# A four-layer graph network on one core: when the experts' weights are turned, and where layer 0's keys, values and context are computed

## The chip, the cores and the metric

The kernel runs on one NeuronCore of a Trainium2 chip. A core has five engines, each with its own in-order queue: TensorE (matmuls; its loads of stationary operands are listed apart as PEld), VectorE (DVE in the profile), ScalarE (ACT), GpSimd (POOL) and SyncE (SP), which here only starts transfers. Sixteen DMA engines move data. The metric is the device time of one execution in microseconds (us).

## The reference

A graph of 3125 nodes with 256 features and 103,125 edges passes through four layers. Each layer normalizes its rows, adds a graph attention and a "mix" (some form of global attention), normalizes again and adds a feed-forward part. Two places matter here.

Layer 0's mix, as this kernel computes it from the normalized rows `xn` and the weight matrix `Wqkv` (256 x 768):

```python
q, k, v = xn @ Wqkv                    # 256 columns each
context = softmax(k over nodes).T @ v  # by head, 32 x 32 in each of 8 heads
gate    = sigmoid(gelu(ln(xn) @ Wg1 + bg1) @ Wg2 + bg2)
x      += (gate * (q @ context)) @ Wproj + bproj
```

The kernel multiplies the query weights with the context once (a 256 x 256 matrix that it calls `fold`), so that `q @ context` is one product `xn @ fold`.

Layer 1's feed-forward part:

```python
shared  = relu(relu(x @ sW1 + sb1) @ sW2 + sb2) @ sW3 + sb3
w       = weights of the top 2 of 4 experts, from softmax(x @ gW + gb)
out     = shared + sum_e w[e] * (relu(relu(x @ eW1[e] + eb1[e]) @ eW2[e] + eb2[e]) @ eW3[e] + eb3[e])
```

## The kernel before

**Tiles.** The 3125 rows lie in 25 tiles of 125 rows (`NT`, `TP`). Tiles are taken in seven `GROUPS`: four of four tiles (500 columns when turned) and three of three (375). `x` holds the rows, `xn` the normalized rows and `xT` the same turned, as two blocks of 128 features by 3125 columns.

**The order of the work.** The code states what depends on what and in which order it is written; a planner then puts the instructions of each engine into a fixed order, by an estimate of when each could start, and by the order in the code where several could. It also places the semaphores. On the chip each engine follows that order strictly: an instruction that waits holds all behind it on its engine. Transfers start from the queues of SP, ScalarE and GpSimd. A pool with `bufs=2` gives a name two buffers in turn, and a third use waits until the first buffer's readers are done. PSUM, where matmuls write, is shared by the pools of a stage.

**The beginning.** `run` (L2479 on) loads `x`, and `begin_layer` normalizes all seven groups and turns them into `xT`. Then `prepare` checks that the graph has a form for which the fast layers hold. VectorE compares the first target of each of 3224 rows of edges with five sets of first nodes (L1381, 125 x 3224 each), and GpSimd gathers 256 edges for each of 625 sets of nodes from memory (five indirect transfers, L1387). VectorE turns these into a low digit and a key for each edge, which go to memory (`seg_d`), counts what it found, bounds the attention scores by products of `xT` with the attention vectors (L1437 to L1439), bounds the key weights (`w_k`), and writes one word `ok`. All engines read `ok` (`values_load`), and a branch takes either the fast layers or a general path. Nothing of the fast layers can be moved before the branch by the planner.

**Layer 0's counts.** `counts` (L1480) builds, for the 625 sets of five nodes, how many edges lead from each node to each. It works in 63 steps of ten sets: VectorE makes two one-hot arrays in bf16 (`oh_lo`, L1515, and `oh_key`, L1518, two buffers each), TensorE multiplies them (`p_cnt`, L1530, 20 matmuls a step), ScalarE copies the counts to bytes (`stage`, L1532), and each 250 columns go to memory. Beside it runs a generator, `mix0_pieces`, of which pieces are taken between the steps:

```python
while done < (g0 // B + 1) * PIECES0 // steps:
    next(work, None)
    done += 1
```

`PIECES0` is 107, just as many as there are: one for the weights, 25 for keys, values and context (one for each tile: a product with 512 columns, exp of the keys, a copy of the values, two context products that add up over all tiles in `p_ctx`), one for `fold`, 42 for the gate and the output (six for each group), and 38 for `node_pieces`, which make the attention's node tables `zs` and `bar` and the queries `q_d`. After the loop, `dense_pairs` reads the counts back (`a`) and multiplies.

**Layer 1's feed-forward.** `ffn1` goes through the groups. `before(i + 1)` turns group i+1 (`transposed`, into `p_tr`), computes its router scores, takes softmax and top 2 on VectorE (some 25 short operations, with ScalarE's exp between), and turns the resulting weights `wf` so that they lie as 5 x 500 (L1056 to L1058). Then group i's shared network runs (`h1`, `h2`), then its four experts in two pairs, each pair masked by a product of `own` with the turned weights (`p_e`, L1086), and at last `p_y`, which adds shared part, experts and biases. `p_tr`, `p_e` and `p_y` have two PSUM buffers each.

Of the kernel before, what the change touches and what calls it, by code (L numbers as in the profile page):

```python
# [10 lines left out]
F32 = mybir.dt.float32  # L11
# [30 lines left out]
KEYS = HI * GN  # L42
PIECES0 = 107
SC = 8
# [5 lines left out]
GROUPS = [(0, 4), (4, 4), (8, 4), (12, 4), (16, 3), (19, 3), (22, 3)]  # L50
# [6 lines left out]
class Net:  # L57
# [976 lines left out]
    def ffn1(self, x, xn, xT, weights):  # L1034
        nc, tc = self.nc, self.tc
        E = 4
        with ExitStack() as s:
            c = s.enter_context(tc.tile_pool(name="f1", bufs=1))
# [4 lines left out]
            wfs = {}  # L1043

            def before(i):
                if i < len(GROUPS):
                    t0, nt = g = GROUPS[i]
                    self.transposed(ps, xT, xn, groups=[g])
                    wf = self.top2(wr, self.softmax(wr, self.scores(wr, ps, xT[:, :, t0 * TP:(t0 + nt) * TP], nt, gw, gb)))

                    more = wr.tile([TP, nt, E + 1], F32, name="wf_1")
                    nc.vector.memset(more[:, :, E:], 1.0)
                    nc.vector.tensor_copy(more[:, :, :E], wf)
                    p = ps.tile([P, 512], F32, name="p_tr")[:E + 1]
                    for t in range(nt):
                        nc.tensor.transpose(p[:, t * TP:(t + 1) * TP], more[:, t, :], self.ident[:TP, :TP])  # L1056
                    wfs[i] = wr.tile([E + 1, 512], F32, name="wf_t")
                    nc.scalar.activation(wfs[i][:, :nt * TP], p[:, :nt * TP], AF.Copy)  # L1058

# [3 lines left out]
            for i, (t0, nt) in enumerate(GROUPS):  # L1063
                before(i + 1)
                wf = wfs[i]
                n = nt * TP
# [8 lines left out]
                self.mm(p[:, :n], [(s2[:, k, :], h1[:, k, :n]) for k in range(KC)])  # L1075
                nc.scalar.activation(h2[:, :n], p[:, :n], AF.Relu, bias=sb2[:, 0:1], scale=1.0)
                pairs = []
                for j in range(E // 2):
# [272 lines left out]
class Dense(Net):  # L1351
# [8 lines left out]
    def prepare(self, pool, xT):  # L1360
# [6 lines left out]
        with ExitStack() as s:  # L1367
# [18 lines left out]
            for b in range(GN):  # L1386
                nc.gpsimd.indirect_dma_start(out=seg[:, b, :], out_offset=None, in_=ins["segments"],  # L1387
                                             in_offset=bass.IndirectOffsetOnAxis(ap=at_i[:, b:b + 1], axis=0))
            lo = w.tile([TP, GN, SEG], F32, name="seg_lo")
            key = w.tile([TP, GN, SEG], F32, name="seg_key")  # L1390
# [37 lines left out]
            nc.vector.tensor_reduce(found[:, 1:2], above, AX.X, OP.add)  # L1428
            p_f = ps.tile([1, 2], F32, name="p_f")
            nc.tensor.matmul(p_f, self.ones[:, 0:1], found, start=True, stop=True)  # L1430


            gw = self.gnn_weight(w, ps, "g0", 8)
            ends = w.tile([16, 2, len(GROUPS)], F32, name="ends")
# [30 lines left out]
            nc.vector.tensor_mul(self.ok, ok[:, 0:1], ok[:, 2:3])  # L1465
        return self.ok

# [4 lines left out]
    def counts(self, pieces):  # L1472
# [5 lines left out]
        with ExitStack() as s:  # L1478
# [5 lines left out]
            with tc.tile_pool(name="cnti", bufs=1) as wi, tc.tile_pool(name="cntt", bufs=2, space=PSUM) as ps:  # L1484
                for i, name in enumerate(("lo_t", "key_t")):
# [57 lines left out]
    def mix0_pieces(self, x, xn, xT, nodes, c, w):  # L1543
# [3 lines left out]
        with ExitStack() as s:  # L1547
            ps = s.enter_context(tc.tile_pool(name="m0p", bufs=3, space=PSUM))
            ps1 = s.enter_context(tc.tile_pool(name="m0p1", bufs=1, space=PSUM))
            wqkv = self.weight(c, "L0_mix_Wqkv")  # L1550
            wproj = self.weight(c, "L0_mix_Wproj")
# [3 lines left out]
            bg1, bg2 = self.vec(c, "L0_mix_bg1", rows=64), self.vec(c, "L0_mix_bg2")  # L1555
            bproj = self.row(c, "L0_mix_bproj")
            nc.gpsimd.tensor_add(x, x, bproj[:, None, :].to_broadcast([TP, NT, C]))
            p_ctx = [ps1.tile([P, P + 1], F32, name=f"p_ctx{m}") for m in range(KC)]
            yield
            for t in range(NT):  # L1560
                p = ps.tile([TP, 2 * C], F32, name="p_a")
                self.mm(p, [(xT[:, k, t * TP:(t + 1) * TP], wqkv[:, k, C:]) for k in range(KC)])
                ek = w.tile([TP, C], F32, name="ek", bufs=2)
                nc.scalar.activation(ek, p[:, :C], AF.Exp)
                v = w.tile([TP, KC, P + 1], F32, name="v", bufs=2)
                nc.scalar.activation(v[:, :, :P], p[:, C:].rearrange("p (m f) -> p m f", m=KC), AF.Copy)
                nc.gpsimd.memset(v[:, :, P], 1.0)
                for m in range(KC):
                    nc.tensor.matmul(p_ctx[m], ek[:, m * P:(m + 1) * P], v[:, m, :], start=(t == 0), stop=(t == NT - 1))
                yield  # L1570

            inv = w.tile([P, KC], F32, name="inv")
            ctxt = w.tile([P, KC, P], F32, name="ctxt")
            for m in range(KC):
                nc.vector.reciprocal(inv[:, m:m + 1], p_ctx[m][:, P:])
                nc.vector.scalar_tensor_tensor(ctxt[:, m, :], p_ctx[m][:, :P], inv[:, m:m + 1], self.heads, op0=OP.mult, op1=OP.mult)
            fold = c.tile([P, KC, C], F32, name="fold")
            for k in range(KC):
                p = ps.tile([P, 512], F32, name="p_a")
                for m in range(KC):  # L1580
                    nc.tensor.transpose(p[:, m * P:(m + 1) * P], wqkv[:, k, m * P:(m + 1) * P], self.ident)
                wt = w.tile([P, C], F32, name="wq_t")
                nc.vector.tensor_copy(wt, p[:, :C])
                p = ps.tile([P, 512], F32, name="p_a")
                for m in range(KC):
                    nc.tensor.matmul(p[:, m * P:(m + 1) * P], wt[:, m * P:(m + 1) * P], ctxt[:, m, :], start=True, stop=True)
                nc.vector.tensor_copy(fold[:, k, :], p[:, :C])
            yield
            for t0, nt in GROUPS:
# [876 lines left out]
    def run(self, x_in, out):  # L2466
# [195 lines left out]
```

## Time and profile before

| | |
|---|---|
| median of 3 runs | 5535.72 us (5531.63 to 5546.36) |
| profiled execution | 5533.53 us, span 5531.5 us |
| mean granted TensorE clock | 0.938 |
| start to `ok` | 92.1 us |
| from `ok` to the end of the counts and node tables | 92.1 to 392.2 us |
| layer 1's feed-forward part | 2682 to 2928 us |

The span runs from the first instruction to the last; the profiled execution's own time is 2.0 us longer. A row of the profile gives source line, engine and operation, then the tiles as output <- input with the partitions and elements of each; idle time before an instruction is put down to the semaphore that came last. `<-issue` is idle time in which nothing visible was waited for. The granted clock is TensorE's, as a share of full speed. A matmul on f32 data appears as two records; the ends of pipelined matmuls are modelled.

### The profile page before, as it was taken

How to read it: one execution, taken by the hardware profiler on the slowest of the kernel's cores; microseconds unless marked ns; L12 is line 12 of the kernel's file. 1: busy time of each engine (PE TensorE's matmuls, PEld its weight loads, DVE VectorE, ACT ScalarE, POOL GpSimd, SP SyncE). 2: the span in 40 equal slices, each digit the busy share in tenths (PEclk: the TensorE clock that was granted, in tenths of full speed). 3: DMA queues.
4: the chain of work that ended last, by engine and by line, in shares of the span. 5: the costliest groups of instructions: out<-in, count | busy, mean ns of one | idle time of the engine just before them, and what ended most of it. 6: DMA issues, size and time to landing. Idle time of an engine off the chain costs nothing. (4 is left out here: it accounts for less than half of the span.)

```text
span 5531.5 us, 66568 instructions
## 1 busy us (share of the span) xinstructions
PE 4813.9 (87%) x24758; PEld 2824.0 (51%) x24758; DVE 3733.4 (67%) x5901; ACT 1034.3 (19%) x1984; POOL 1041.6 (19%) x1185
## 2 busy tenths in 40 slices
PE   4978888879788899989889899979998878989878
PEld 2652234448645433368544433345565555655557
DVE  7789999985565699845333899932223888777753
ACT  2540010011142100110123000023333110333221
POOL 1000000004300000000001100000001777777743
PEclk7999999989899999999889999979999888999989
DMA  3462222232300011111000011120002556666645
GB/s 87 36 68 67 77 63 67 67 116 63 99 19 0 27 34 41 32 39 36 24 1 4 28 33 34 26 71 0 0 1 59 161 164 193 183 173 178 175 149 170
DMA packets 294339, 395.81 MB, mean 72 GB/s; under 512 B 124175, under 2 KB 228000, under 8 KB 293435
## 3 DMA queue, kind: packets, MB, share of 16 engines
q1 hardware_dynamic: 203408, 161.12, 12.7%
q0 software_dynamic: 52528, 167.17, 10.7%
q10 hardware_dynamic: 38072, 63.16, 3.6%
q8 instruction: 202, 3.31, 0.3%
q14 instruction: 129, 1.06, 0.1%
HBM read 345.14 MB, written 49.35 MB: 71 GB/s over the span
## 5 line engine op out<-in xcount | busy, mean ns | idle before, releaser
L1699 DVE SCALAR_TENSOR_TENSOR pt<-q_head,bar,a 128x750 f32<-128x750 f32 (+5 forms) x1200 | 1483.3, 1298 | 80.4 <-PE acc L1804 57.3
L1954 POOL DMA_INDIRECT z_edge<-tab,src_i x806 | 778.0, 965 | 266.9 <-issue 206.4
L1748 PE MATMUL acc<-pt,zs 128*64 128x500 f32 (+2 forms) x2800 | 591.1, 548 | 152.0 <-DVE pt L1699 127.2
L1799 PE MATMUL acc<-pt,zs 128*64 128x375 f32 (+2 forms) x3200 | 604.9, 501 | 25.4 <-DVE pt L1699 25.0
L2022 PE MATMUL p_acc<-z_edge,oh 128*125 128x264 f32 x2044 | 539.9, 425 | 91.7 <-DVE z_edge L2013 91.7
L2022 PEld LDWEIGHTS p_acc<-z_edge,oh 128*125 128x125 f32 x2044 | 419.8, 209 | 191.3 <-DVE z_edge L2013 101.2
L1748 PEld LDWEIGHTS acc<-pt,zs 128*64 128x64 f32 (+1 forms) x2800 | 244.4, 136 | 483.3 <-DVE pt L1699 328.7
L1799 PEld LDWEIGHTS acc<-pt,zs 128*64 128x64 f32 (+1 forms) x3200 | 244.9, 136 | 362.0 <-issue 224.7
L1215 DVE SCALAR_TENSOR_TENSOR x<-p_y,sm,x 125x256 f32<-125x256 f32 x200 | 93.9, 484 | 427.0 <-PE p_y L716 427.0
L1804 PE MATMUL acc<-pt,zs 128*32 128x375 f32 (+2 forms) x3200 | 313.4, 497 | 0.0
L1850 PE MATMUL acc<-zs,pt 128*125 128x257 f32 x1250 | 275.7, 383 | 11.8 <-DMA a<-count_d 11.8
L1850 PEld LDWEIGHTS acc<-zs,pt 128*125 128x125 f32 x1250 | 234.8, 189 | 52.7 <-issue 14.6
L2013 DVE TENSOR_TENSOR z_edge<-z_edge,near_e 128x2112 f32<-128x2112 f32 (+1 forms) x101 | 236.5, 2342 | 17.4 <-ACT near_e L2005 17.4
L1210 ACT ACTIVATE h<-p_tr,bn 128x500 f32<-128x500 f32 (+1 forms) x224 | 161.5, 722 | 357.6 <-PE p_tr L716 357.6
L716 PE MATMUL p_y<-w_L_ffn_Wo,h 128*125 128x256 f32 x800 | 203.7, 387 | 0.0
L1699 DVE SCALAR_TENSOR_TENSOR pt<-q_all,bar,a 128x500 f32<-128x500 f32 (+3 forms) x175 | 119.0, 682 | 122.9 <-PE acc L1850 120.4
L716 PE MATMUL p_tr<-h,w_L_ffn_W 128*128 128x500 f32 (+1 forms) x448 | 191.6, 551 | 7.8 <-ACT h L1210 4.7
L2362 POOL CAST one_e<-one 125x96 bf16<-125x96 f32 (+1 forms) x2 | 2.1, 1049 | 1013.5 <-DVE one L653 1013.5
L716 PE MATMUL p_tr<-xT,w_L_ffn_W 128*128 128x500 f32 (+1 forms) x448 | 190.0, 547 | 0.0
L1804 PEld LDWEIGHTS acc<-pt,zs 128*32 128x32 f32 (+1 forms) x3200 | 85.0, 109 | 203.0 <-issue 201.7
L716 PEld LDWEIGHTS p_y<-w_L_ffn_Wo,h 128*125 128x125 f32 x800 | 144.9, 187 | 73.4 <-ACT h L1210 27.1
L1967 DVE TENSOR_TENSOR hot<-row,near 125x1024 f32<-125x1024 int16 (+1 forms) x149 | 157.6, 1083 | 4.5 <-DMA row<-dst_row 2.9
(513 smaller groups left out, 6696.0 us busy)
## 6 DMA issues: line engine op xcount, KB each, us to landing
row<-dst_row SPq DMA_DIRECT2D x101, 224.0 KB
a<-count_d SPq DMA_DIRECT2D x96, 203.1 KB
a<-count_d SPq DMA_DIRECT2D x96, 187.5 KB
a<-count_d SPq DMA_DIRECT2D x144, 93.8 KB
ef<-in_edge_s SPq DMA_DIRECT2D x101, 128.0 KB
z_edge<-tab,src_i POOLq DMA_INDIRECT x806
count_d<-stage SPq DMA_DIRECT2D x12, 781.2 KB
q_head<-q_g ACTq DMA_DIRECT2D x24, 375.0 KB
```

What stands on the lines that cost most here:

```text
L716: self.nc.tensor.matmul(p, a, b, start=(i == 0), stop=(i == len(pairs) - 1))
L1210: nc.scalar.activation(o[:, m, :n], p[:, :n], AF.Relu, bias=b[:, e, m:m + 1], scale=g[:, e, m:m + 1])
L1215: nc.vector.scalar_tensor_tensor(x[:, t0 + t, :], q, wf[:, t, e:e + 1], x[:, t0 + t, :], op0=OP.mult, op1=OP.add)
L1699: self.nc.vector.scalar_tensor_tensor(pt[:K, :n], q, bar, a[:K, :n], op0=OP.max, op1=OP.mult)
L1748: nc.tensor.matmul(acc[64 * i:64 * i + 64, :b1 - b0], zs[:K, t, z:z + 64], pts[i][:K, b0:b1], start=(t == 0), stop=(t == NS - 1))
L1799: nc.tensor.matmul(acc[i // 2][64 * (i % 2):64 * (i % 2) + 64, b, :b1 - b0], zs[:K, t, i * W:i * W + 64], pts[i][:K, b0:b1], **st)
L1804: nc.tensor.matmul(acc[2][32 * i:32 * i + 32, b, :b1 - b0], zs[:K, t, z:z + 32], pts[i][:K, b0:b1], **st)
L1850: nc.tensor.matmul(acc[i], pt[:K, i * TP:(i + 1) * TP], zs[:K, t, :C + 1], start=(t == 0), stop=(t == NS - 1))
L1954: nc.gpsimd.indirect_dma_start(out=zs[i][:, j, :], out_offset=None, in_=table, in_offset=bass.IndirectOffsetOnAxis(ap=src[:, c0 + j:c0 + j ...
L1967: nc.vector.tensor_tensor(hots[i, t][:, q0 * 256:q1 * 256], rows[i][:, q0 * 256:q1 * 256], node[:, t:t + 1].to_broadcast([TP, (q1 - q0) * ...
L2013: nc.vector.tensor_mul(zh, zh, weight[:, :, :, None].to_broadcast([P, n, H, D + 1]))
L2022: nc.tensor.matmul(acc[t], ohs[i, t][:, k - a, :], zs[i][:, k - c0, :HW], start=(k == cols[t][0]), stop=(k == cols[t][1] - 1))
```

## The change

Four edits.

1. In `ffn1` the turning of the router's weights (transposes, and the copy by ScalarE) leaves `before(i + 1)` and becomes `turned(i)`, called behind group i's shared network.
2. A new function `begin` takes the place of `begin_layer` and the call of `prepare` in `run`. `prepare` is now a generator with two stops. `begin` runs it to the first stop (the gathers), then normalizes and turns group by group, and computes keys, values and context for each group's tiles; after the third group's turning it runs `prepare` to its second stop. Then come `fold`, which is written to memory, and the rest of `prepare`.
3. `mix0_pieces` loses keys, values, context and `fold`, and reads `fold` from memory. `PIECES0` becomes 69, while 81 pieces are left, so that 12 follow the loop. PSUM pools `cntp` and `m0p` go from three buffers to four.
4. In `mix0_pieces` the scaled copy of the turned rows `xnnT` goes from VectorE to ScalarE.

```diff
-PIECES0 = 107
+PIECES0 = 69
...
@@ ffn1, in before(i)
-                    more = wr.tile([TP, nt, E + 1], F32, name="wf_1")
-                    nc.vector.memset(more[:, :, E:], 1.0)
-                    nc.vector.tensor_copy(more[:, :, :E], wf)
-                    p = ps.tile([P, 512], F32, name="p_tr")[:E + 1]
-                    for t in range(nt):
-                        nc.tensor.transpose(p[:, t * TP:(t + 1) * TP], more[:, t, :], self.ident[:TP, :TP])
-                    wfs[i] = wr.tile([E + 1, 512], F32, name="wf_t")
-                    nc.scalar.activation(wfs[i][:, :nt * TP], p[:, :nt * TP], AF.Copy)
+                    wfs[i] = wr.tile([TP, nt, E + 1], F32, name="wf_1")
+                    nc.vector.memset(wfs[i][:, :, E:], 1.0)
+                    nc.vector.tensor_copy(wfs[i][:, :, :E], wf)
+
+            def turned(i):
+                nt = GROUPS[i][1]
+                p = ps.tile([P, 512], F32, name="p_tr")[:E + 1]
+                for t in range(nt):
+                    nc.tensor.transpose(p[:, t * TP:(t + 1) * TP], wfs[i][:, t, :], self.ident[:TP, :TP])
+                wf = wr.tile([E + 1, 512], F32, name="wf_t")
+                nc.scalar.activation(wf[:, :nt * TP], p[:, :nt * TP], AF.Copy)
+                return wf
...
                 before(i + 1)
-                wf = wfs[i]
...
                 nc.scalar.activation(h2[:, :n], p[:, :n], AF.Relu, bias=sb2[:, 0:1], scale=1.0)
+                wf = turned(i)
...
@@ prepare: a stop behind the five gathers, another ahead of p_f; p_f and p_gw take the name p_e
+            yield
...
+            yield
-            p_f = ps.tile([1, 2], F32, name="p_f")
+            p_f = ps.tile([1, 2], F32, name="p_e")
...
-            gw = self.gnn_weight(w, ps, "g0", 8)
+            gw = self.gnn_weight(w, ps, "g0", 8, "p_e")
...
+    def begin(self, pool, x, xn, xT):
+        nc, tc = self.nc, self.tc
+        self.fold_d = self.dram.tile([P, KC * C], F32, name="fold_d")
+        with ExitStack() as s:
+            c = s.enter_context(tc.tile_pool(name="c0", bufs=1))
+            w = s.enter_context(tc.tile_pool(name="c0w", bufs=2))
+            pst = s.enter_context(tc.tile_pool(name="c0t", bufs=2, space=PSUM))
+            ps = s.enter_context(tc.tile_pool(name="c0p", bufs=2, space=PSUM))
+            ps1 = s.enter_context(tc.tile_pool(name="c0c", bufs=1, space=PSUM))
+            checks = self.prepare(pool, xT)
+            next(checks)
+            wqkv = self.weight(c, "L0_mix_Wqkv")
+            p_ctx = [ps1.tile([P, P + 1], F32, name=f"p_ctx{m}") for m in range(KC)]
+            self.layernorm(xn, x, GROUPS[0])
+            for i, (t0, nt) in enumerate(GROUPS):
+                self.transposed(pst, xT, xn, groups=[GROUPS[i]])
+                if i + 1 < len(GROUPS):
+                    self.layernorm(xn, x, GROUPS[i + 1])
+                if i == 2:
+                    next(checks)
+                for t in range(t0, t0 + nt):
+                    p = ps.tile([TP, 2 * C], F32, name="p_a")
+                    self.mm(p, [(xT[:, k, t * TP:(t + 1) * TP], wqkv[:, k, C:]) for k in range(KC)])
+                    ek = w.tile([TP, C], F32, name="ek")
+                    nc.scalar.activation(ek, p[:, :C], AF.Exp)
+                    v = w.tile([TP, KC, P + 1], F32, name="v")
+                    nc.scalar.activation(v[:, :, :P], p[:, C:].rearrange("p (m f) -> p m f", m=KC), AF.Copy)
+                    nc.gpsimd.memset(v[:, :, P], 1.0)
+                    for m in range(KC):
+                        nc.tensor.matmul(p_ctx[m], ek[:, m * P:(m + 1) * P], v[:, m, :], start=(t == 0), stop=(t == NT - 1))
...
+            nc.sync.dma_start(self.fold_d, fold.rearrange("p k f -> p (k f)"))
+            for _ in checks:
+                pass
...
@@ counts
-            ps = s.enter_context(tc.tile_pool(name="cntp", bufs=3, space=PSUM))
+            ps = s.enter_context(tc.tile_pool(name="cntp", bufs=4, space=PSUM))
...
@@ mix0_pieces: the 25 tiles of keys, values and context and the making of fold are gone
-            wqkv = self.weight(c, "L0_mix_Wqkv")
...
+            fold = c.tile([P, KC, C], F32, name="fold")
+            nc.sync.dma_start(fold.rearrange("p k f -> p (k f)"), self.fold_d)
...
-                    nc.vector.tensor_scalar(xnnT[:, k, :n], p[:, :n], g[:, k:k + 1], b[:, k:k + 1], op0=OP.mult, op1=OP.add)
+                    nc.scalar.activation(xnnT[:, k, :n], p[:, :n], AF.Identity, bias=b[:, k:k + 1], scale=g[:, k:k + 1])
...
@@ run
-        self.begin_layer(x, xn, xT)
-        ok = nc.values_load(self.prepare(pool, xT)[0:1, 0:1], min_val=0, max_val=1)
+        self.begin(pool, x, xn, xT)
+        ok = nc.values_load(self.ok[0:1, 0:1], min_val=0, max_val=1)
```

What is left out inside `begin` is the making of `inv`, `ctxt` and `fold`, line for line as it stood in `mix0_pieces`.

More of the change, by code (lines that the diff above doesn't have):

```diff
@@ L1465, in prepare @@
             nc.vector.tensor_mul(self.ok, ok[:, 0:1], ok[:, 2:3])
-        return self.ok
+    def begin(self, pool, x, xn, xT):
[28 more added lines that the diff above has]
+                        nc.tensor.matmul(p_ctx[m], ek[:, m * P:(m + 1) * P], v[:, m, :], start=(t == 0), stop=(t == NT - 1))
+            inv = c.tile([P, KC], F32, name="inv")
+            ctxt = c.tile([P, KC, P], F32, name="ctxt")
+            for m in range(KC):
+                nc.vector.reciprocal(inv[:, m:m + 1], p_ctx[m][:, P:])
+                nc.vector.scalar_tensor_tensor(ctxt[:, m, :], p_ctx[m][:, :P], inv[:, m:m + 1], self.heads, op0=OP.mult, op1=OP.mult)
+            fold = c.tile([P, KC, C], F32, name="fold")
+            for k in range(KC):
+                p = ps.tile([P, 512], F32, name="p_a")
+                for m in range(KC):
+                    nc.tensor.transpose(p[:, m * P:(m + 1) * P], wqkv[:, k, m * P:(m + 1) * P], self.ident)
+                wt = w.tile([P, C], F32, name="wq_t")
+                nc.vector.tensor_copy(wt, p[:, :C])
+                p = ps.tile([P, 512], F32, name="p_a")
+                for m in range(KC):
+                    nc.tensor.matmul(p[:, m * P:(m + 1) * P], wt[:, m * P:(m + 1) * P], ctxt[:, m, :], start=True, stop=True)
+                nc.vector.tensor_copy(fold[:, k, :], p[:, :C])
+            nc.sync.dma_start(self.fold_d, fold.rearrange("p k f -> p (k f)"))
+            for _ in checks:
+                pass
@@ L1547, in mix0_pieces @@
         with ExitStack() as s:
-            ps = s.enter_context(tc.tile_pool(name="m0p", bufs=3, space=PSUM))
-            ps1 = s.enter_context(tc.tile_pool(name="m0p1", bufs=1, space=PSUM))
-            wqkv = self.weight(c, "L0_mix_Wqkv")
+            ps = s.enter_context(tc.tile_pool(name="m0p", bufs=4, space=PSUM))
             wproj = self.weight(c, "L0_mix_Wproj")
@@ L1556, in mix0_pieces @@
             bproj = self.row(c, "L0_mix_bproj")
+            fold = c.tile([P, KC, C], F32, name="fold")
+            nc.sync.dma_start(fold.rearrange("p k f -> p (k f)"), self.fold_d)
             nc.gpsimd.tensor_add(x, x, bproj[:, None, :].to_broadcast([TP, NT, C]))
[L1558 to L1587, printed above, removed]
             yield
```

## The prediction

> **What bounds the kernel now.** I read the page first, then busy time by stretch, then the waits and the order of time inside the two stretches that the diff touches.
>
> ```profile
> PE 4813.9 (87%) x24758; PEld 2824.0 (51%) x24758; DVE 3733.4 (67%) x5901; ACT 1034.3 (19%) x1984; POOL 1041.6 (19%) x1185
> ```
> TensorE leads, but this is an average. By stretch (columns: length, then busy PE, PEld, DVE, ACT, POOL, granted clock, DMA):
> ```profile
> 40.00:54.00 14.00, 0.00 (x0) 0.00 (x0) 14.00 (x14) 0.00 (x0) 0.00 (x0) 0.50 0.00 0
> 2682.00:2928.00 246.00, 204.27 (x656) 106.38 (x657) 74.36 (x328) 67.65 (x110) 0.64 (x3) 0.84 0.02 7
> 3700.00:4240.00 540.00, 529.45 (x1796) 310.92 (x1795) 134.00 (x361) 171.19 (x243) 0.46 (x1) 1.00 0.00 1
> ```
> The checks at the start are VectorE alone. Layer 1's experts (2682 to 2928) lose TensorE time at clock 0.84, while a stretch that is 98% busy has 1.00. The waits of TensorE in 2682 to 2928, and one turn in order of time:
> ```profile
> PE p_tr L1056 <- DVE wf L1053: 40.5, 7, 6.3
> ```
> ```profile
> 2744.85 0.99 PE L1056 MATMUL p_tr<-ident,wf 125*5 125x125 f32 x4 [5.99 <-DVE wf L1053]
> 2745.64 5.91 PE L716 MATMUL p_tr<-xT,w_L_ffn_sW 128*128 128x500 f32 x8
> ...
> 2753.25 3.52 PE L716 MATMUL p_tr<-xT,w_L_ffn_eW 128*128 128x500 f32 x8
> ```
> TensorE stands 6 us before it can turn the router's weights, seven times; then eight matmuls take 5.91 us, where eight of the same shape a little later take 3.52.
>
> The counting loop of layer 0 (same columns), and its first stretch's wait:
> ```profile
> 132.00:200.00 68.00, 66.26 (x489) 45.04 (x489) 47.18 (x40) 39.89 (x96) 1.92 (x19) 1.00 0.49 36
> 200.00:290.00 90.00, 84.37 (x561) 56.95 (x559) 76.41 (x89) 45.97 (x79) 0.00 (x0) 0.96 0.37 28
> 290.00:382.00 92.00, 88.43 (x733) 65.91 (x732) 83.32 (x94) 57.21 (x123) 0.00 (x0) 1.00 0.65 50
> ```
> ```profile
> DVE oh_lo L1515 <- PE p_cnt L1530: 25.4, 9, 5.2
> ```
> TensorE bounds it; VectorE waits for it while keys and values run. Its ends, in order of time:
> ```profile
> 66.19 1.49 DVE L1392 CAST rel<-seg 125x1280 f32<-125x1280 int32 x1 [7.40 <-DMA seg<-in_segments,at_i]
> ...
> 92.14 0.15 DVE L1465 TENSOR_TENSOR ok<-ok_f 1x1 int32<-1x1 f32 x1
> ```
> ```profile
> 400.94 16.26 SPq L1706 DMA_DIRECT2D a<-count_d  x6
> 406.31 1.78 DVE L1699 SCALAR_TENSOR_TENSOR pt<-q_head,bar,a 128x1500 f32<-128x1500 f32 x1 [13.94 <-DMA a<-count_d]
> ```
> Nothing of layer 0 starts before `ok`. After the last count, 24.3 us (382 to 406.3) go to writing the counts and reading them back.
>
> **What the Trainium skill says.** "TensorE: Matmul & The Clock Gate", "What's actually happening": the clock halves after an idle window of about 3.4 us and returns after as long a busy one. The trace agrees: idle of 6 us, then 0.83 us a matmul for 5 us, then 0.42. "ScalarE: Activation LUTs", "What ACT_TABLE_LOAD costs": 1283 ns a load; the trace has 1.28. "GPSIMD Engine Reference", "Specifications": GpSimd shares its SBUF interfaces with VectorE's two-input operations; here two key one-hots took 11.7 us beside GpSimd's 13.7 us addition instead of 2.9. "Perfetto Trace Analysis", "Identifying the Most-Contended Engine": matmul busy is a poor measure of room, so I cost TensorE by distances between starts.
>
> **Part 1, the experts' weights.** Nothing is removed: 25 transposes and 7 copies move from before group i's shared network to behind it, a group later than their VectorE chain, which then has some 25 us for its 6.
> - Waits gone: 40.5 us.
> - Slow clock gone. First shared layer, 8 matmuls, six times: 5.97, 5.91, 5.84, 4.58 against 3.52 and 4.90, 4.95 against 2.79: 12.5 us. Six sets of turning transposes (0.99 against about 0.55): 2.5. Second layer (2.03 against 1.87): 0.8. After the first wait, transposes 1.96 for 1.07, scores 3.64 for 1.91, a mask product 2.03 for 1.10: 3.5. Sum 19.3.
> - New: the turning takes a p_tr buffer (two in all), so the first expert's product waits for h2's ScalarE copy, 0.68 us against 0.4 us of transposes: say 0.4 x 7 = 3 (between 0 and 7). Behind that wait stand the experts' products, then p_y.
> Sum -57 us (between -45 and -61). The next layer starts from this stretch's last addition, so it passes to the end.
>
> **Part 2, the counting loop.** Removed from 132 to 382: about 20 of 25 tiles of keys, values and context. A tile costs (66.3 - 24.3 for counts - 1.5 for the fold) / 19.75 = 2.05 us of TensorE; in this stretch and with the fold some 46 us. TensorE 239 - 46 = 193; of this, 12 of 81 pieces now come after the loop (69 are spread over it), some 8 us, so 185. VectorE 206.9 - 8.8 (the row of L1600 has 9.7 in 14, less some 0.07 by which neighbours overlap) - 2.2 (fold) = 196. The bound changes engine. At 93% busy, between the 90.6% and 96% of the stretch 290 to 382, 196 / 0.93 = 210 against 250: -40 (at 96%: -46; at 88%: -27).
> ScalarE gains 14 scaled copies, 0.79 and 0.69 us by the skill's 280 + 93 + 0.833 N ns (L1611's 0.675 is the near row), 10 us, and loses 15 of keys and values and two to four table loads: 143 becomes about 133 of 210, hidden; uncovered it would cost up to 10.
> Start of the loop, 93.4 to 132: VectorE's 5.2 us wait behind TensorE's keys goes, and 768 KB of weights become 256 KB of fold, about 2: -7. GpSimd's addition stays.
> The 12 late pieces (8 us TensorE, then 9 us of scaling zs) lie in the 24.3 us of count write and read; uncovered they cost 8. More PSUM buffers: nothing, no long wait names them.
>
> **Part 3, the beginning.** Added: 768 KB on SP's queue behind x and the row heads (3.2 + 1.6 + 0.4 + 0.8 MB at the 265 to 286 GB/s that the trace shows from 8 to 20 us: lands near 25 us); 25 tiles x 2.05 = 52; fold 2; a 256 KB write on SP behind the seg writes, for which nothing waits before the gate. TensorE then: 25 + 52 + scores' ends 10.5 (16 x 0.42 + 12 x 0.32) + leftovers of transposes, fold and gw 5 = 93, then 3.5 us from last product to `ok` as now, plus 4 for waits: 100 against 92. VectorE: 7.3 + 80 now + 3 fold = 90 if the 7.4 us gap is filled, so it isn't last. GpSimd gets 25 memsets of 0.1 us in one queue with the five gathers (1.3 each): whichever waits holds the other, and behind a late gather stand the context products. ScalarE gets 20 us and at most 14 table loads, 18 us, of 85. Cost +8 (0 to +25).
>
> Sum: -57 - 40 - 7 + 8 = -96. The profiled execution took 5533.5 (span 5531.5); the median shown is 2.2 higher. So 5437.5 profiled, **5440** as a median.
>
> **Rivals.**
> - The beginning eats the loop's gain: gathers and memsets block each other, or keys run only after the scans (54 us), ending `ok` near 140. For: a memset behind GpSimd's addition held TensorE 7.5 us here. Against: the planner can put ready work first. Only part 1 counts: 5479.
> - The experts' wait only moves: turned weights late for the mask product, or p_tr's two buffers stall the experts 6 us a group. Against: the chain is one group early. Parts 2 and 3 stay, half of part 1 goes: 5468.
> - Slower, by the clock: if denser TensorE work lowered the granted clock throughout, each 1% of 4814 us costs 48; 96 us are gone at 2%, a mean of 0.92 instead of 0.938, and at 0.91 it takes 5585. Against: 3700 to 4240 held 1.00 at 98% busy.
> - The planner puts the moved work back where it was: 5536.
>
> **How the numbers follow.** Forecast 0.68 (own range 5418 to 5465), first rival 0.15, second 0.11, clock 0.02, no change 0.04. The range 5418 to 5482 holds the forecast but its edges, and the first two rivals in most of their spread. A measurement tells 0.3% (17 us) from no change: faster 0.94, same 0.04, slower 0.02.
>
> **What would show it.** Part 1: no wait of some 6 us at the turning transposes, the first shared layer at 3.5 us, stretch near 189 us. Part 2: VectorE above 90% busy in the loop, no long waits of oh_lo for p_cnt, first pt near 365. Part 3: TensorE busy from about 25 us, `ok` near 100; table loads by the group. Wrong if `ok` passes 125, if TensorE still leads in the loop, or if the experts' stretch stays above 215.

## The result, and the profile after

| | before | after |
|---|---|---|
| median | 5534.91 us (5531.63 to 5546.36, 4 runs) | 5462.52 us (5460.73 to 5465.36, 4 runs) |
| ratio, 95% interval | | 0.9868 (0.9857 to 0.9880) |
| profiled execution, span | 5533.53, 5531.5 us | 5463.07, 5461.2 us |
| mean granted clock | 0.938 | 0.945 |

The kernel is 72.4 us faster (1.3%); 96 had been forecast. Line numbers after the first thousand have moved: `oh_lo` is L1574, `oh_key` L1577, `p_cnt` L1589, the first weighing of pairs (`pt`) L1728.

The page's first part, and busy time by stretch (length, then busy PE, PEld, DVE, ACT, POOL, granted clock, DMA share, GB/s) of the kernel after:
```profile
PE 4806.4 (88%) x24758; PEld 2817.3 (52%) x24758; DVE 3723.4 (68%) x5887; ACT 1046.3 (19%) x2000; POOL 1041.7 (19%) x1185
```
```profile
40.00:54.00 14.00, 7.85 (x22) 4.56 (x22) 13.15 (x30) 7.88 (x15) 4.41 (x4) 0.76 0.11 26
...
169.00:260.00 91.00, 84.04 (x710) 61.02 (x709) 89.00 (x82) 59.94 (x112) 0.00 (x0) 0.98 0.58 45
260.00:364.00 104.00, 97.07 (x858) 72.69 (x857) 101.09 (x105) 68.11 (x143) 0.00 (x0) 0.98 0.65 52
364.00:393.00 29.00, 6.17 (x31) 3.50 (x30) 9.30 (x26) 4.24 (x11) 0.00 (x0) 0.65 1.00 138
```
The page hardly differs from that of before. The stretches do: beside the checks (40 to 54) TensorE now works, but only 7.85 of 14 us and at clock 0.76. In the counting loop VectorE is 97% busy (190.1 of 195 us) and TensorE 93% (181.1), so TensorE no longer leads.

**Layer 1's experts.** The stretch, TensorE's waits in it, and one turn in order of time:
```profile
2669.50:2857.90 188.40, 183.25 (x655) 96.50 (x655) 71.32 (x326) 66.26 (x110) 0.34 (x2) 0.97 0.03 9
```
```profile
PE p_tr L716 <- ACT h L1079: 2.8, 6, 1.1
...
PE p_y L716 <- ACT h L1079: 0.8, 1, 0.8
```
```profile
2736.78 1.08 PE L716 MATMUL p_tr<-xT,w_L_ffn_sW 128*128 128x500 f32 x2
...
2739.14 2.76 PE L716 MATMUL p_tr<-xT,w_L_ffn_sW 128*128 128x500 f32 x6
...
2743.62 0.59 PE L1059 MATMUL p_tr<-ident,wf 125*5 125x125 f32 x4
2744.55 3.62 PE L716 MATMUL p_tr<-xT,w_L_ffn_eW 128*128 128x500 f32 x8 [0.34 <-ACT h L1079]
```
The wait for `wf` (40.5 us) is gone. The shared layer's eight matmuls take 1.08 + 2.76 us instead of 5.91, the four transposes 0.59 instead of 0.99. In place of the wait stands the small one that was named, for ScalarE's `h2`: 2.8 us in all. Before, this stretch took 245.7 us (2682.2 to 2927.9), so it gives 57.3.

**Beginning, loop and what follows it.** VectorE's order of time:
```profile
60.42 1.49 DVE L1397 CAST rel<-seg 125x1280 f32<-125x1280 int32 x1 [7.23 <-DMA seg<-in_segments,at_i]
...
124.72 0.15 DVE L1471 TENSOR_TENSOR ok<-ok_f 1x1 int32<-1x1 f32 x1
...
139.64 13.97 DVE L619 TENSOR_SCALAR xnn<-xn,mv,rstd 125x256 f32<-125x256 f32 x4
```
```profile
384.58 0.27 DVE L1699 TENSOR_SCALAR es<-es 128x200 f32<-128x200 f32 x1 [13.75 <-ACT es L1698]
...
392.95 27.15 DVE L1728 SCALAR_TENSOR_TENSOR pt<-q_head,bar,a 128x1500 f32<-128x1500 f32 x16
```
ScalarE's queue ahead of that `es` (ACTq are transfers that it starts):
```profile
383.29 0.36 ACTq L1763 DMA_DIRECT2D q_head<-q_g  x1
383.70 0.37 ACT L1697 ACTIVATE bar<-es 128x200 f32<-128x200 f32 x1 [13.05 <-DMA count_d<-stage]
```
And VectorE's wait in the loop that was 25.4 us in its first stretch alone:
```profile
DVE oh_lo L1574 <- PE p_cnt L1589: 4.0, 3, 2.1
```
`ok` comes at 124.9 instead of 92.3, though the gathered edges arrive 5.8 us earlier than before (60.4 against 66.2). From there the loop runs faster: the last key one-hot ends at 364.1 instead of 382.9. The first weighing, at 392.95, no longer waits for the counts but for the node tables, which are scaled behind two exps of ScalarE. The balance against the spans:

| stretch | before | after | difference | forecast |
|---|---|---|---|---|
| start to `ok` | 92.3 | 124.9 | +32.6 | +8 |
| `ok` to the end of the last key one-hot | 290.6 | 239.2 | -51.4 | -47 |
| from there to the first weighing | 23.4 | 28.9 | +5.5 | 0 |
| layer 1's experts | 245.7 | 188.4 | -57.3 | -57 |
| sum | | | -70.6 | -96 |

The spans differ by 70.3 us; after the experts the lead over the kernel before wanders between 63.5 and 70.3, so that small differences elsewhere cancel. Of what is missing to the forecast 24.6 us lie in the beginning and 5.5 behind the loop; the loop gave 4.4 more than forecast.

**What held the beginning.** TensorE, ScalarE and GpSimd of the kernel after, in order of time (an `<-` in brackets names what ended the idle time); ahead of them VectorE's scan that they stand behind:
```profile
36.87 3.55 DVE L1385 TENSOR_SCALAR_CACHE_REDUCE below_n<-heads_f,first_node 125x3224 f32<-125x3224 f32 x1
...
40.35 0.18 DVE L614 BATCH_NORM_AGGREGATE mv<-bn_st 125x2 f32<-125x6 f32 x1
```
```profile
40.56 0.30 ACT L616 ACTIVATE rstd<-mv,eps 125x3 f32<-125x3 f32 x1 [6.02 <-DVE mv L614]
40.87 1.28 ACT L1500 ACT_TABLE_LOAD   x1
42.17 0.38 ACT L1500 ACTIVATE ek<-p_a 125x256 f32<-125x256 f32 x1
```
```profile
42.97 1.20 PE L1505 MATMUL p_ctx<-v,ek 125*128 125x129 f32 x4 [6.10 <-ACT v L1502]
...
56.48 1.23 PE L1505 MATMUL p_ctx<-v,ek 125*128 125x129 f32 x4 [5.67 <-POOL v L1503]
...
70.98 1.88 PE L716 MATMUL p_a<-w_L_mix_Wqkv,xT 128*125 128x512 f32 x4
72.91 0.68 PE L1505 MATMUL p_ctx<-v,ek 125*128 125x129 f32 x4
73.43 1.88 PE L716 MATMUL p_a<-w_L_mix_Wqkv,xT 128*125 128x512 f32 x4
```
```profile
48.68 1.59 POOL L1391 DMA_INDIRECT seg<-in_segments,at_i  x1 [14.14 <-DVE xn L619]
```
Read it as one chain over four queues. VectorE has five scans of 3.54 to 3.56 us from 29 to 48, and between them one or two short operations of a normalization at a time (`mv`, a mean and a variance, is one). ScalarE waits for these with a square root at the head of its queue; behind the root stand the exps of tiles already multiplied; behind the exps TensorE waits with the context product. At 48.7 GpSimd starts five gathers, and the column of ones for the next tile stands behind them until 56. Only from 66 on does TensorE run without a gap, and then a tile takes 73.43 - 70.98 = 2.45 us. By then eight of 25 tiles were done.

### The profile page after: what moved, and what is told of

The parts are those of the page before. It is cut to its first block, busy times and chain, and to the rows that moved or that the text cites. A ratio compares the mean times of both kernels' runs of the same rounds, so it can differ in the third digit from the quotient of the medians.

```text
span 5461.2 us, 66541 instructions
## 1 busy us (share of the span) xinstructions
PE 4806.4 (88%) x24758; PEld 2817.3 (52%) x24758; DVE 3723.4 (68%) x5887; ACT 1046.3 (19%) x2000; POOL 1041.7 (19%) x1185
## 3 DMA queue, kind: packets, MB, share of 16 engines
q0 software_dynamic: 52528, 167.17, 10.8%
## 5 line engine op out<-in xcount | busy, mean ns | idle before, releaser
L1728 DVE SCALAR_TENSOR_TENSOR pt<-q_head,bar,a 128x750 f32<-128x750 f32 (+5 forms) x1200 | 1482.6, 1295 | 66.1 <-PE acc L1833 57.7
L2051 PE MATMUL p_acc<-z_edge,oh 128*125 128x264 f32 x2044 | 537.6, 424 | 92.3 <-DVE z_edge L2042 92.3
L1728 DVE SCALAR_TENSOR_TENSOR pt<-q_all,bar,a 128x500 f32<-128x500 f32 (+3 forms) x175 | 119.0, 682 | 123.0 <-PE acc L1879 120.7
```

Of the source, the lines that this page charges most:

```text
L1728: self.nc.vector.scalar_tensor_tensor(pt[:K, :n], q, bar, a[:K, :n], op0=OP.max, op1=OP.mult)
L2051: nc.tensor.matmul(acc[t], ohs[i, t][:, k - a, :], zs[i][:, k - c0, :HW], start=(k == cols[t][0]), stop=(k == cols[t][1] - 1))
```

## The experiments

Two chips were used, named A and B here. The chip of the first result is not on record; it is counted as A, because the kernel before took 5534.9 us there, 5536.9 on A and 5813 to 5815 on B. On B the last layers (from 4200 us on) take some 300 us longer for every kernel and whole times vary by up to 36 us between runs; up to 4000 us the marks agree with A's to some microseconds. Whole times are therefore compared within a chip, and most verdicts rest on marks of the trace. Column "loop from" is the third `oh_lo`, from which the loop runs at its own pace; "last" the start of the last `oh_key`. Each mark is that of one profiled execution. Five profiles have the same work ahead of `ok` (after, after again, bias on TensorE, 77 pieces, xnnT back), and it comes at 123.4 to 124.7 in them.

| kernel | chip | `ok` | loop from | last | first weighing | median, us | ratio to before |
|---|---|---|---|---|---|---|---|
| before | A | 92.1 | 132.0 | 382.1 | 406.3 | 5534.9 | |
| after | A | 124.7 | 168.8 | 363.3 | 392.95 | 5462.5 | 0.9868 |
| after, again | B | 123.4 | 166.7 | 358.7 | 384.3 | 5758.0 | 0.9893 |
| experts alone | B | 91.5 | 133.0 | 379.6 | 402.25 | 5772.2 | 0.9917 |
| ends by group | B | 119.8 | 165.9 | 358.0 | 384.95 | 5738.8 | 0.9879 |
| ones ahead | B | 117.4 | 161.2 | 353.7 | 379.9 | 5739.3 | 0.9869 |
| norms ahead | B | 128.1 | 171.6 | 362.7 | 388.2 | 5750.1 | 0.9885 |
| norms, ones, xT | A | 113.1 | 156.5 | 349.3 | 376.2 | 5452.9 | 0.9849 |
| the same and ends | A | 104.0 | 150.2 | 342.7 | 368.6 | 5445.4 | 0.9831 |
| bias on TensorE | A | 124.5 | 156.1 | 356.7 | 383.4 | 5460.3 | 0.9861 |
| 77 pieces | A | 123.5 | 166.8 | 363.6 | 384.9 | 5458.6 | 0.9860 |
| xnnT back | B | 124.3 | 169.6 | 372.4 | 398.8 | 5766.3 | 0.9912 |
| free chain, 77 | B | 106.5 | 152.4 | 347.9 | 369.1 | 5740.4 | 0.9860 |
| the same and bias early | B | 100.5 | 133.2 | 328.9 | 350.5 | 5713.3 | 0.9814 |

The run of the kernel after on chip B:

> The changed kernel as it is, beside the three below on the same chip, so that they can be compared with it and not only with the kernel before. All theories: ok at 124 to 125, first weighing at 391 to 395, ratio to before 0.987.

`ok` at 123.4 and a ratio of 0.9893 (0.9865 to 0.9920), whose interval holds the 0.987 that was expected. The first weighing came at 384.3, earlier than expected: the counts' writes and what waits for them were done at 374.7 instead of 383.3. From the end of the last key one-hot to the first weighing it was 24.8 us here and 28.9 there, with one kernel; differences below some 8 us in the column "first weighing" say nothing between chips, and with one profile of each kernel little within a chip.

**Part 1 alone.**
```diff
 kernel before, ffn1 only
-    wfs[i] = wr.tile([E + 1, 512], F32, name="wf_t")   # turned in before(i)
+    wf = turned(i)                                     # turned behind h2
```


> The kernel before with the first edit alone (the experts' weights turned behind the shared network). If the parts add up: the experts' stretch falls from 246 to 189 us, nothing else moves, and the time is 5535 - 57 = 5478. Rival: part of the 57 us came from a higher clock that other parts brought along; then only the 40.5 us of waits go and it takes some 5495.

The stretch of this kernel on chip B:
```profile
2681.50:2869.90 188.40, 183.18 (x655) 96.60 (x655) 71.41 (x326) 66.21 (x110) 0.36 (x2) 0.97 0.03 9
```
188.4 us at clock 0.97, the very figures of the full change. The clock came back with the wait, not with other parts. The whole time fell by 41 us (the ratio's interval is 35 to 62 us of 5813), less sharp than the stretch, but well away from nothing. Against this run the full change's first weighing is 17.9 us earlier on the same chip: parts 2 and 3 together are worth about that (13.4 between the first two profiles, whose chip is taken as A).

**What holds the beginning: three single edits.** First the scores' ends by group:
```diff
     self.transposed(pst, xT, xn, groups=[GROUPS[i]])
+    self.group_ends(i)          # p_e product, max and min of this group
```


> The changed kernel, with the products that bound the scores, and their maxima and minima, written for each group right behind that group's turning instead of behind all keys, values and fold. Theory 'order' (TensorE stands idle for some 25 us before 62 us, and this work could have been done there): the word ok is written near 113 instead of 124.9, time 5462.5 - 11 = 5451. Rival 'TensorE is full' (what is moved only pushes the keys back by as much): ok stays at 122 to 125, time 5460 to 5463.

Second the ones for `v`:
```diff
+vs = [c.tile([TP, KC, P + 1], F32, name=f"v{i}") for i in range(2)]
+for v in vs:
+    nc.gpsimd.memset(v[:, :, P], 1.0)
...
-nc.gpsimd.memset(v[:, :, P], 1.0)
```


> The changed kernel, with the columns of ones in two standing buffers for v, set once ahead of the loop over tiles, so that GpSimd does nothing for a tile. Rival 'GpSimd' (memsets and gathers hold each other, and the memset that waits for the context products makes a tile take 2.45 us): a tile takes some 2.05 us, the 5.7 us wait behind the gathers goes, ok near 109, time 5447. Theory 'order': tiles keep 2.45 us because TensorE is without a gap from 66 to 108 us, and only some of the 5.7 us at 56 goes: ok at 119 to 124, time 5457 to 5462.

Third the normalizations:
```diff
+for g in GROUPS:
+    self.layernorm(xn, x, g)
 checks = self.prepare(pool, xT)
 next(checks)
-...  self.layernorm(xn, x, GROUPS[i + 1])
```


> The changed kernel, with all seven normalizations written ahead of the checks' first part, so that VectorE's five scans come behind them. Theory 'order' (the scans between the normalizations hold ScalarE's square roots, behind them its exps, and so TensorE, until 62): tiles run at 2.45 us from about 28, the last context product is near 96 instead of 108.6, ok near 112, time 5450. Rival 'GpSimd': the gathers now come later still and hold the memsets longer; ok not before 122, time 5460 or more.

Against 123.4 on the same chip, `ok` moved by -3.6, -6.0 and +4.7 us. None gave the `ok` that the theory of mere order had forecast. With the ends by group the last context product moved from 107 to 117, so most of what was moved pushed the keys back: the rival "TensorE is full" is nearer. With the ones ahead a tile takes 2.38 us where it had taken 2.45; the memset does not set the pace, as the theory of order had it. But the wait behind the gathers is real (6.6 us in the kernel after on that chip), and 6 us go, 1.6 more than that theory allowed. With the normalizations ahead, `ok` at 128.1 is where the rival had put it (122 or later), though not by the gathers alone. TensorE's waits were these:
```profile
PE p_a L716 <- DVE xT L294: 13.5, 3, 5.3
PE p_ctx L1504 <- POOL v L1502: 3.8, 1, 3.8
```
Every second copy of turned rows goes through VectorE, and now it was these that stood behind the scans, while the gathers, later by 2.7 to 3.7 us, held the ones as before. Moving one piece of check work handed the hold to the next queue. The theory had to be widened: a tile's chain must not cross the queues of VectorE and GpSimd at all.

**The chain freed.**
```diff
 (normalizations ahead, ones ahead, and)
-self.transposed(pst, xT, xn, groups=[GROUPS[i]])
+for k in range(KC):             # the same transposes
+    ...
+    nc.scalar.activation(xT[:, k, t0 * TP:(t0 + nt) * TP], ..., AF.Copy)
```


> The changed kernel with three edits in its beginning: all normalizations ahead of the checks' first part, ones for v set once in two standing buffers, and all copies of turned rows xT on ScalarE. A tile's keys, values and context then cross only TensorE and ScalarE. Theory 'crossed queues' (each hold before 62 us came from an instruction standing in VectorE's or GpSimd's queue behind check work, and moving one piece of it, as in the run with the normalizations ahead, only brings the next hold): TensorE runs from 26 us at 2.45 us a tile, last context product near 26 + 61 + 6 for turning = 93 (108.6 in the changed kernel), then the scores' ends as now, some 16: ok near 109. Rival 'table loads and ScalarE' (ScalarE with 14 copies more becomes what a tile waits for): a tile takes over 2.6 us and ok stays above 115.

> As the run with normalizations, ones and copies of xT moved, and the scores' ends by group too. Theory 'crossed queues' with a full TensorE: last context product near 93 + 8 = 101, and ok some 3 us behind it, near 104. Rival: the maxima and minima now stand in VectorE's queue among the scans, and p_e has two buffers, so TensorE waits for them: ok at 108 or later, no better than without this edit.

In the first of the two the last context product came at 97.6 and `ok` at 113.1, each four to five later than expected; a tile took 2.38 us, so ScalarE does not set the pace. Its one long wait of TensorE between 20 and 115 us:
```profile
PE p_e L1436 <- DVE found L1421: 12.3, 1, 12.3
```
A product of the checks stood in TensorE's queue ahead of ready keys. With the ends by group too, no wait of over 1.3 us was left ahead of `ok`, which came at 104.0, as expected:
```profile
103.95 0.15 DVE L1475 TENSOR_TENSOR ok<-ok_f 1x1 int32<-1x1 f32 x1
```
That is 20.8 us earlier than in the change, and 17 us in the median (5445.4 against 5462.5, on the same chip but not beside each other). Here it is TensorE's own work that ends last: 25 tiles of 2.38, the ends and the turning.

**The loop's bound.** The fourth edit undone (`xnnT` by `nc.vector.tensor_scalar` again):

> The changed kernel with its fourth edit undone: the scaled copy of xnnT on VectorE again (14 operations of 0.63 us on average, 8.8 us, beside the loop). If VectorE bounds the loop (97% busy from 168 to 360, TensorE 93%), the stretch from the third oh_lo to the last key one-hot goes from 194 to some 203 us, first weighing near 402, time 5471. Rival: TensorE or the two together set the pace and VectorE had room: less than 3 us.

The loop from the third `oh_lo` to the end of the last `oh_key`, of the kernel after on chip B:
```profile
166.70:359.50 192.80, 180.19 (x1567) 133.87 (x1566) 189.97 (x186) 128.21 (x254) 0.00 (x0) 0.99 0.57 50
```
and with the copy on VectorE:
```profile
169.60:373.20 203.60, 183.34 (x1568) 137.47 (x1566) 198.19 (x199) 120.38 (x242) 0.00 (x0) 0.96 0.54 48
```
VectorE has 8.2 us more to do and the loop takes 10.8 more, where seven profiles with the loop of the kernel after lie within 191.9 to 195.2 us. VectorE bounds the loop. The median rose by 8.3 us, but the two kernels' times overlap (5741.8 to 5773.1 against 5752.9 to 5760.7) and show nothing by themselves.

**The start of the loop.** GpSimd's addition left out, its bias added by TensorE:
```diff
-nc.gpsimd.tensor_add(x, x, bproj[:, None, :].to_broadcast([TP, NT, C]))
...
-self.mm(p[:, i, :], [(gate.., wproj..) for m in range(KC)])
+self.mm(p[:, i, :], [(gate.., wproj..) for m in range(KC)] + [(self.ones[:1, :TP], bproj[:1, :])])
```


> The changed kernel without GpSimd's addition of the output bias to all of x (13.7 us at the loop's start); TensorE adds the bias as a third product (one row of ones by the bias) in each output product. Theory: the four normalizing operations of xnn, 13.97 us beside that addition, take 1.4 us, and the third oh_lo comes some 11 us earlier against ok (33 instead of 44 us after ok): first weighing of pairs near 382 instead of 393, time 11 us shorter, less at most 4 for 50 short products. Rival: the start waits for something else (digits and keys of edges from memory), and the third oh_lo stays within 3 us of 44 after ok.

The same four operations as in the third line of VectorE's order of time above:
```profile
139.07 1.35 DVE L619 TENSOR_SCALAR xnn<-xn,mv,rstd 125x256 f32<-125x256 f32 x4
```
1.35 us instead of 13.97, and the loop begins 31.5 us after `ok` instead of 44.1: the addition had held VectorE. How it held it shows when the row of the kernel after is taken apart:
```profile
138.85 13.65 POOL L1616 TENSOR_TENSOR x<-x,r_L_mix_bproj 125x6400 f32<-125x6400 f32 x1 [10.16 <-DMA r_L_mix_bproj<-in_L_mix_bproj]
```
```profile
139.64 13.01 DVE L619 TENSOR_SCALAR xnn<-xn,mv,rstd 125x256 f32<-125x256 f32 x1
```
One of the four operations began 0.8 us after the addition and ended 0.15 us after the addition's end; the other three took 0.40 each, as ever. They are not slowed by a factor: the first waits for the end of the addition, and VectorE's whole queue behind it.

Of the 12.6 us gained here 6 to 9 were lost again in the loop, which took 201.5 us instead of 192.8 to 195.2. (First weighing came at 383.4, where 382 had been expected; with 384.3 and 392.95 in the two profiles of the kernel after, that shows little.) The 50 records of the third product cost TensorE 17.3 us, and it became the busier engine of the loop (195.0 us, VectorE 191.4):
```profile
L716 PE MATMUL p_a<-r_L_mix_bproj,ones 1*125 1x256 f32 x50 | 17.3, 425 | 0.0
```
A record over one row took 425 ns on average, one of the products over 128 rows beside it (also 256 columns) 402. The price expected for it (4 us) was four times too low.

**The pieces behind the loop.** `PIECES0 = 77` instead of 69:

> The changed kernel with PIECES0 = 77 instead of 69: all node tables and both exps of es come within the loop, only the four pieces of scaling zs behind it. Theory: the exps no longer stand in ScalarE's queue behind transfers of q_head that wait for the counts' writes, so VectorE scales zs while the counts are written and read, and the stretch from the last key one-hot to the first weighing goes from 29.6 to some 25 us; TensorE's 8 pieces fit beside VectorE. First weighing near 389, 4 us gained. Rival: the loop takes the eight pieces at their full price and is 5 to 8 us longer, net 0 to 4 us lost.

From the start of the last key one-hot to the first weighing it took 21.3 us (25.6 and 29.7 without the edit); the node tables were scaled by 375 and the weighing waited 10.1 us for the counts, as before the change. But the loop took 197.6 us instead of 192.8 to 195.2. First weighing at 384.9, and 384.3 in the repeat of the change without this edit: nothing gained, which is nearer the rival.

**Together.** The freed chain with 77 pieces, and the same with the bias added in the beginning (by GpSimd, behind the normalizations; the general path takes it off again):
```diff
 if i == 2:
     next(checks)
+    bproj = self.row(c, "L0_mix_bproj")
+    nc.gpsimd.tensor_add(x, x, bproj[:, None, :].to_broadcast([TP, NT, C]))
...
 with either.Else():
+    nc.vector.tensor_sub(x, x, bproj[:, None, :].to_broadcast([TP, NT, C]))
```


> The beginning freed as in the run with normalizations, ones, copies of xT and scores' ends moved, and PIECES0 = 77. If the two gains are separate (one ahead of the loop, one behind it): ok near 104, from the last key one-hot to the first weighing some 21 us, first weighing near 361, 32 us ahead of the changed kernel's 393; time 5431 by the changed kernel's 5462.5. Rival: the earlier end of the beginning was paid back behind the first weighing (there the first such run lost 12.5 us between 1130 and 1230 us, where the clock was at half): then 5440 to 5447.

> As the run before, with the bias added to x by GpSimd in the beginning, behind the normalizations, instead of at the loop's start (the other branch takes it off again). Theory: VectorE has some 20 us to spare in the beginning, so that ok moves by less than 5 us, and the third oh_lo comes 32 instead of 44 us after ok: first weighing near 351, time 5422. Rival: the addition holds VectorE's scans by its 13.7 us, the gathers and all behind them come later, ok at 112 or later, and nothing or less than 5 us is gained over the run before.

The first reached 369.1 instead of the expected 361, no better than the freed chain alone (368.6): the 77 pieces again gave nothing that can be told from noise. Nothing was paid back later (from the first weighing to the first turned rows of layer 0's routed experts 847.8 us, 847.6 in the change). The second came at 350.5, where 351 was expected, and in part by luck: the start of the loop gave 13.3 us, for 12 expected, but `ok`, at 100.5, also came 6 us earlier than in the first. That was not forecast, and its cause was not tried; in the first, TensorE waited 4.1 us for the weights of keys and values, in the second it did not. GpSimd's addition lay beside VectorE's scans and did not hold them:
```profile
29.14 15.32 POOL L1508 TENSOR_TENSOR x<-x,r_L_mix_bproj 125x6400 f32<-125x6400 f32 x1 [24.62 <-DVE xn L619]
```
```profile
34.45 3.57 DVE L1385 TENSOR_SCALAR_CACHE_REDUCE below_n<-heads_f,first_node 125x3224 f32<-125x3224 f32 x1
...
38.53 3.55 DVE L1385 TENSOR_SCALAR_CACHE_REDUCE below_n<-heads_f,first_node 125x3224 f32<-125x3224 f32 x1
```
The addition itself took 15.32 us instead of 13.65. A cast of VectorE had begun 0.2 us before it and ran for the first 1.7 us of it, so here it may have been GpSimd that waited; that was not tried.

This version beats both kernels: 5713.3 us where the change took 5758.0 and the kernel before 5815.2, beside each other on chip B (0.9814, 0.9786 to 0.9842, against 0.9893).

## Why the prediction was right, and where it was off

**Part 1: right in size and cause.** The stretch gave 57.3 us for 57, and the new wait for `h2` came to 2.8 + 0.8 us for 3. That the slow clock went with the wait, and not with another part, is shown by the run with part 1 alone. The rival in which the wait only moves is out.

**Part 2: right, the loop a little better than forecast, its start not.** The engine that bounds did change, as the run with `xnnT` back shows. VectorE's share was put at 93%, and it was 97%. From `ok` to the last key one-hot 51.4 us went, for 47 forecast. Not as forecast was the start of the loop: -7 had been set down, and it grew from 39.8 to 44.1 us. The prediction kept GpSimd's addition and its price as they were, and read that price as a slowing ("two key one-hots took 11.7 us ... instead of 2.9"). It is a wait for the addition's end: in the kernel before, one of the two one-hots stood for 10.33 us, until 1.3 us after that end, and the other took 1.46. In the kernel after, the planner put a normalizing operation there, which met the addition near its beginning and stood for 13.01. Some of what the loop then gained are normalizations that had been done in this start. One sum was loose: 20 tiles of 2.05 us and 2 for the fold are 43 us off TensorE, not 46; as VectorE bounds the loop, nothing hangs on it. ScalarE's 14 copies took 0.66 to 0.78 us each, for 0.69 and 0.79 priced. What the fourth PSUM buffers did was not tried.

**The 12 late pieces: the cover failed in part.** They were put at nothing, with 8 if uncovered. Their matmuls were covered. The scaling was not: ScalarE's exps stand in its queue behind the transfers of `q_head`, and these wait for writes that run behind those of the counts. So VectorE scaled from 384.6 to 392.9, when the counts were there. The prediction costed the pieces by engine and did not follow ScalarE's queue, in which transfers and work share one order.

**Part 3: the step that failed.** "100 against 92" became 124.9 against 92.3, just inside the bound of 125 that was named as the sign of error. The cost, "+8 (0 to +25)", became +32.6 and left its own range. Two of its terms were off:
- "25 tiles x 2.05 = 52": a tile takes 2.45, thus 61, 10 us more. 2.05 had been a remainder, what was left of TensorE's busy time beside the counts. But the records overlap: in that very stretch (132 to 200 us) the tiles' products cover 35.6 us, their contexts 14.0 and the counts 24.4, 74 us in all where TensorE is busy for 66.3. So 2.05 prices a tile that lies beside the counts, and one that runs without them takes more.
- "plus 4 for waits": up to 65.4 us TensorE finished 8 tiles, 19.6 us of work at 2.45 each, in the 38.9 us since its first keys (26.5). Some 19 us went to waits, to turning and to the clock that the waits brought down (0.76 from 40 to 54). Freed of them, and with the ends moved in between, the same work reached `ok` at 104.0 and 100.5.

The term that was missing is the queue, not the engine. The prediction added up TensorE's and VectorE's work in the beginning, found 93 and 90, and took the larger. With 61 us for the tiles TensorE's sum becomes 102, and with the chain freed `ok` did come near that, at 104.0. In the change neither sum bound `ok` alone, because each tile crossed four queues in which check work stood ahead of it. The first rival ("the beginning eats the loop's gain") named the gathers and memsets, worth 6 us of it, and keys that run only behind the scans, which happened to the context of 21 of 25 tiles. The truth lay between that rival (5479) and the forecast (5440), at 5462.5. That this is inside the range is owed to the range's width, not to the account of part 3.

**The clock.** The rival in which denser work lowers the mean clock is out: 0.945 against 0.938.

How the 19 us divide between scans, copies and gathers was not settled; the single edits don't add up (-3.6, -6.0 and +4.7 against -20.8 for all with the copies).

## What to carry to other kernels

When work is laid beside other work, don't add up engines; follow one unit of it through every queue that it crosses and ask what stands ahead of it there, transfers included. Moving one blocker hands the hold to the next queue: free the whole chain or expect little. And where a long addition on GpSimd must run, look at which VectorE operations meet it: some stand until it ends, with all that is queued behind them, and others run as if it were not there.

## What the runs showed of the hardware

- Beside GpSimd's addition one VectorE operation stands until the addition has ended. In ten of the twelve profiles with that addition in the loop's start it is a normalizing operation, which ends 0.13 to 0.15 us after it (12.90 to 13.83 us instead of 0.4); in the other two (before, experts alone) it is a key one-hot, which has two inputs (10.33 and 9.85 us instead of 1.46). Scans with an accumulator are not held (3.55 to 3.57 us with and without the addition), nor are statistics and reciprocals. "GPSIMD Engine Reference", "Key points", of the Trainium skill says that the engines contend where VectorE has a two-port mode or two inputs in SBUF; the one-hot fits the second. That passage does not by itself say why, of normalizing operations and scans, both with one tensor and scalars for each partition, only the first are held; no run tried it.
- The clock fell without an idle window. In the freed chain's profile, from 1138 to 1170 us (columns as above):
```profile
1138.00:1142.00 4.00, 4.00 (x17) 2.19 (x15) 1.66 (x5) 0.79 (x3) 0.00 (x0) 1.00 1.10 362
1142.00:1146.00 4.00, 3.29 (x9) 1.78 (x8) 3.19 (x11) 2.11 (x7) 0.00 (x0) 0.69 0.96 321
1146.00:1158.00 12.00, 12.00 (x25) 6.28 (x24) 4.52 (x13) 4.97 (x9) 0.00 (x0) 0.50 1.06 338
1158.00:1170.00 12.00, 11.16 (x24) 5.92 (x25) 5.44 (x18) 1.39 (x5) 0.00 (x0) 0.50 0.14 45
```
  One wait of 0.7 us, and the clock is at half for the next 24 us although TensorE is busy. The same work ran at 1.00 in the kernel after (1162 to 1178). "TensorE: Matmul & The Clock Gate", "What's actually happening", of the skill gives an idle window of some 3.4 us for such a fall, and as long a busy one for the return; this stretch agrees with neither. It cost that execution some 12 us (98 instead of 85 to 86 from the last product of pairs to the routed experts). It was seen in one execution; the cause was not tried.
